# A two-layer decoder on one core: the order of TensorE, VectorE and ScalarE taken from the source instead of the scheduler

## The chip, the core and the metric

The kernel runs on one core of a Trainium2 chip. The core has several engines that run side by side, each with its own list of instructions: TensorE (PE; matmuls and transposes, with its weight loads listed apart as PEld), VectorE (DVE), ScalarE (ACT), GpSimd (POOL) and SyncE (SP, which here issues most of the transfers). Each works through its own list and waits on the others through semaphores. The metric is the time on the device in microseconds (us), and the lower it is, the better.

## The reference

The input is x, four sequences of 512 tokens with 512 features: 2048 tokens, which the kernel holds as 16 tiles of 128 tokens in 32-bit floats. There is a context of 4 × 512 × 256 and a position for each token. Two layers of three sub-layers follow one another, each with its residual and a layer normalisation after it:

```python
x = layernorm(x + L0_attn(x))         # 64 heads of 8, softmax attention
x = layernorm(x + L0_xattn(x, ctx))   # attention of the context with itself, applied to x
x = layernorm(x + L0_ffn(x))          # 8 experts, 2 a token, a shared expert and a core product
x = layernorm(x + L1_attn(x))         # 16 heads of 128, 4 key heads, rotary, causal
x = layernorm(x + L1_xattn(x, ctx))   # 32 heads of 16, rotary by position
x = layernorm(x + L1_ffn(x))          # gate, up and down with weights rounded to -1, 0, 1
```

The last sub-layer quantises activations too. Its core:

```python
def _quant_act(x):
    s = jnp.max(jnp.abs(x), axis=-1, keepdims=True) / 127.0 + EPS
    return jnp.clip(jnp.round(x / s), -128.0, 127.0), s

gate = jax.nn.silu(_qlinear(x, w_gate))      # 512 -> 2048
up = _qlinear(x, w_up)                       # 512 -> 2048
return _qlinear(gate * up, w_down)           # 2048 -> 512
```

Here `_qlinear` multiplies the rounded activations by the rounded weights and then by both scales, so the largest absolute value of a token's whole row has to be known before its row can be rounded and multiplied.

## The kernel before, in words

The whole program is one function, `decoder_kernel`, with nested functions for the stages. It opens pools of buffers and then issues the stages in turn. It is written for a tile framework: the source calls operations on tiles, and the framework finds which operation depends on which and sets the waits. It also has a scheduler, which chooses each engine's order from the operations that are ready; in the kernel before nothing limits it, so that the order in which an engine runs its instructions is the scheduler's and differs from the source's in places. The transfers of SP follow the operations that they belong to.

The stages, with the lines that matter below:

- **l0_attn** (16 pairs of a batch and two heads at a time on a strip): scores of the next pair, transposes of this one and projections of the one after are interleaved by hand in the source. At the end of a batch come `add_projection` (matmuls at L160, additions into the residual at L292) and `layernorm` (L219 and L220 statistics of four tiles, L222 the square root on ACT, L223 the reciprocal, L226 four normalisations on DVE).
- **l0_xattn**, for each batch: project the context to queries (evacuated at L431 by DVE) and keys, `softmax_scores` (L347 to L349 and the like), transpose the residual, transpose the probabilities, `add_projection`, `layernorm`.
- **l0_ffn**: routing for each batch with many small DVE operations, lists of tokens for each expert in DRAM, then the experts. After them the expert results are gathered by POOL (L817) into rows, `core(2)` and `core(3)` add the core product of two batches (L292), and `finish(b)` adds a token's two results, ACT's L827 and then DVE's L828, before the up-projection and `layernorm`. `finish(0)` runs before the next stage and the other three inside it.
- **l1_attn**: 64 heads in turn. In the source, head n issues for i = 0..3 the scores of head n+1 (matmul L900, mask L901, maxima L902, exponential L904 on ACT), one query matmul of head n+2 (L887), and one transpose group of head n (L917, copied out by DVE at L920 or ACT at L922); then `values` (four matmuls L932). The rotation of a query takes three DVE operations, L857 to L859, and one of POOL, L860, which the scores of the next head but one wait for. Every fourth head has a key matmul too, and every fourth an output projection.
- **l1_xattn**: 128 steps in the source, with two halves each. A step issues first-pass scores five steps ahead (L1116, L1132 are the two kinds of score matmul), their row maxima on DVE (L1120), exponentials on ACT (L1136) and values (L1143). A plan in the source puts all other work at a step and one of three places in it (EARLY, MIDDLE, LATE): rotations (POOL L1097, L1099), projections, the layer normalisation of a finished batch, and the quantisation of the last stage's weights: sums L998 on DVE, roundings L1016 on DVE, L1017 on POOL, L1018 on ACT, one half chunk at a time.
- **l1_ffn**: for each of 16 tiles `first(t)` and `second(t)`, issued by `pipelined` as first(0), first(1), second(0), first(2), second(1) and so on.

Of the last stage the source is, cut to what issues instructions, with the profile's line numbers:

```python
# first(t)
quantize(X[t], tmp(), xq, s)     # DVE L1305 max, L1306, L1308, L1309 round; ACT L1310 to bf16
flipped(xqt, xq, 4)              # PE L1316 four transposes; DVE L1317 copy
for n in range(4):
    mm(pg, ...); mm(pu, ...)     # PE L160, four matmuls each
    A.activation(g, pg, AF.Silu, scale=gs)                              # ACT L1334
    V.scalar_tensor_tensor(h[n], pu, us, g, ALU.mult, ALU.mult)         # DVE L1335
# second(t)
for n in range(4): V.tensor_reduce(part[:, n:n + 1], h[n], ...)         # DVE L1341
# L1342 to L1344: three small DVE operations
for n in range(4): V.tensor_scalar(h[n], ...); A.activation(hq[:, n, :], ...)   # DVE L1347, ACT L1348
flipped(hqt, hq, 16)             # PE L1316 16 transposes; DVE L1317 four copies
mm(po, chunks(hqt), wd)          # PE L160, 16 matmuls
V.scalar_tensor_tensor(X[t], po, ds, X[t], ...)                         # DVE L1355
```

After every fourth tile a `layernorm` and four stores to the output follow.

Of the kernel before, what the change touches and what calls it, by code (L numbers as in the profile page):

```python
# [85 lines left out]
@with_exitstack  # L86
def decoder_kernel(ctx: ExitStack, tc: tile.TileContext, a: dict, out: bass.AP):
    nc = tc.nc
    wp = ctx.enter_context(tc.tile_pool(name="weights", bufs=10))
    xp = ctx.enter_context(tc.tile_pool(name="resid", bufs=1))  # L90
    cp = ctx.enter_context(tc.tile_pool(name="const", bufs=1))
# [1304 lines left out]
def build(arrays):  # L1396
    import concourse.bacc as bacc

    nc = bacc.Bacc("TRN2", target_bir_lowering=False, num_devices=1)
    args = {k: nc.dram_tensor(f"in_{k}", v.shape, mybir.dt.from_np(v.dtype), kind="ExternalInput").ap()  # L1400
            for k, v in arrays.items()}
    out = nc.dram_tensor("out_0", (T, F), F32, kind="ExternalOutput").ap()
    with tile.TileContext(nc) as tc:
        decoder_kernel(tc, args, out)
    return nc
# [9 lines left out]
```

## Time and profile before

| | |
|---|---|
| time, three runs | 3037.61 us median (3037.56 to 3045.76) |
| the profiled execution: its time, its span | 3051.64 us, 3049.9 us |
| mean granted clock of TensorE | 0.967 |
| busy: PE, DVE, ACT, POOL | 2851.6, 1770.6, 1061.9, 342.5 us |
| instructions in the span | 30386 |
| HBM read, written | 82.76 MB, 46.92 MB |

The profile is of one execution; its span is the time from the first to the last recorded instruction, and its own time is 14 us above the median. Busy times count what an engine executes, without waiting. The granted clock is what the throttle gave TensorE, as a share of full speed.

In the lines quoted below, a group reads: line, engine, operation, what it writes and from what, shape, number, then busy time and mean ns of one, then the idle time of the engine just before these instructions and what ended most of it. A timeline line reads: start in us, us until the end of the last of them, engine, line, operation, shape, number, and in brackets the idle time before and what ended it. A stage's line reads: the stretch and its length, busy time and number of instructions of PE, weight loads, DVE, ACT and POOL, the clock granted, and the share and rate of the transfers.

### The profile page before, as it was taken

Reading aid. Unit: us, or ns where it says so; the run is one execution under the profiler, and the core shown is the slowest. Engines: PE = TensorE matmul, PEld = TensorE weight load, DVE = VectorE, ACT = ScalarE, POOL = GpSimd, SP = SyncE. Lnnn points to the kernel's source line nnn. Section 1 sums busy time; section 2 is a strip of 40 time slices with the busy share of each in tenths; the row PEclk is TensorE's granted clock in tenths of the full one; section 3 lists DMA queues with packets and bytes.
Section 4 is the critical chain, followed back from the end, with each engine's and each line's share of the span. In section 5 each row is a group of like instructions: output and inputs, shape, how many; then the busy total and the mean of one; then the engine's idle time right before and its main releaser. Section 6 shows DMA issues by size and latency. Waiting matters only on the chain.

```text
span 3049.9 us, 30386 instructions
## 1 busy us (share of the span) xinstructions
PE 2851.6 (93%) x11514; PEld 1370.0 (45%) x11514; DVE 1770.6 (58%) x3585; ACT 1061.9 (35%) x1945; POOL 342.5 (11%) x294
## 2 busy tenths in 40 slices
PE   7999998998798899999999999999899998998988
PEld 3444444565455345545545555533233343332444
DVE  4565455443111477757766766755655655564898
ACT  2343243233112222323322232334545444444444
POOL 3000000042002201101100100111212012110000
PEclk9999998989999899999999999999899898999999
DMA  9600001013312120000000001200201100000000
GB/s 374 266 15 1 18 11 35 11 39 115 122 38 77 55 83 1 1 1 1 1 1 1 1 28 35 90 1 15 90 1 42 63 1 28 1 15 1 1 28 28
DMA packets 56454, 131.85 MB, mean 43 GB/s; under 512 B 4810, under 2 KB 24027, under 8 KB 50147
## 3 DMA queue, kind: packets, MB, share of 16 engines
q1 hardware_dynamic: 53218, 121.31, 10.9%
q0 software_dynamic: 3072, 8.39, 0.8%
q8 instruction: 99, 1.62, 0.2%
q14 instruction: 65, 0.52, 0.1%
HBM read 82.76 MB, written 46.92 MB: 43 GB/s over the span
## 4 chain that ended last, share of the span: by engine, by line
PE 52%; DVE 10%; POOL 2%; issue 2%; DMA 1%; ACT 1%; POOLq 0%; DVEq 0%; ACTq 0%; SPq 0%
PE ps_m L160 19%; PE ps_b L1116 7%; PE ps_m L887 6%; PE ps_s L900 5%; PE ps_m L1143 4%; PE ps_b L1132 2%; PE ps_t L917 2%; PE ps_m L932 2%; POOL q L860 1%; DVE maxes L1120 1%; DVE P L1335 1%; PE ps_m L1095 1%; DMA w<-in_L_ffn_downT 1%; PE ps_s L160 1%; DVE tmp L859 1%
## 5 line engine op out<-in xcount | busy, mean ns | idle before, releaser
L160 PE MATMUL ps_m<-w,attnT 128*128 128x512 f32 (+2 forms) x1216 | 446.0, 517 | 12.3 <-issue 8.0
L1120 DVE TENSOR_REDUCE maxes<-ps_b 128x2 f32<-128x1024 f32 x256 | 311.1, 1222 | 244.5 <-PE ps_b L1132 223.6
L1136 ACT ACTIVATE PT<-ps_b 128x1024 f32<-128x1024 f32 x256 | 261.5, 1024 | 313.5 <-PE ps_b L1132 312.9
L1132 PE MATMUL ps_b<-q,k 32*128 32x512 f32 x1024 | 306.4, 678 | 33.3 <-DVE maxes L1120 33.3
L1116 PE MATMUL ps_b<-k,q 32*128 32x512 f32 x1024 | 310.3, 665 | 0.9 <-DVE maxes L1120 0.5
L160 PEld LDWEIGHTS ps_m<-w,attnT 128*128 128x128 f32 x960 | 182.9, 193 | 193.0 <-issue 177.3
L887 PE MATMUL ps_m<-xT,w 128*128 128x512 f32 x512 | 260.3, 592 | 0.0
L292 DVE TENSOR_TENSOR x<-x,ps_m 128x512 f32<-128x512 f32 x128 | 88.0, 688 | 247.5 <-PE ps_m L160 244.6
L904 ACT ACTIVATE P<-ps_s,nmax 128x512 f32<-128x512 f32 (+3 forms) x256 | 135.2, 529 | 233.5 <-DVE nmax L902 232.4
L900 PE MATMUL ps_s<-k,q 128*128 128x512 f32 (+3 forms) x512 | 183.4, 441 | 18.4 <-POOL q L860 18.1
L1116 PEld LDWEIGHTS ps_b<-k,q 32*128 32x128 f32 x1024 | 87.1, 193 | 177.4 <-issue 141.0
L860 POOL TENSOR_TENSOR q<-tmp 128x512 f32<-128x512 f32 x64 | 81.3, 1270 | 750.8 <-DVE tmp L859 714.8
L932 PE MATMUL ps_m<-PT,v 128*128 128x512 f32 (+3 forms) x512 | 162.0, 439 | 2.4 <-DVE PT L920 2.3
L349 ACT ACTIVATE P<-ps_s,nmax 128x512 f32<-128x512 f32 x128 | 88.5, 693 | 204.1 <-DVE nmax L347 204.1
L1143 PE MATMUL ps_m<-PT,vv 128*32 128x512 f32 x1024 | 148.8, 655 | 5.8 <-ACT PT L1136 5.7
L160 PE MATMUL ps_m<-w,xT 128*128 128x512 f32 (+1 forms) x384 | 144.8, 533 | 8.1 <-DVE xT L235 4.2
L911 DVE TENSOR_SCALAR P<-P,sums 128x512 f32<-128x512 f32 (+3 forms) x256 | 145.5, 571 | 4.6
L932 PEld LDWEIGHTS ps_m<-PT,v 128*128 128x128 f32 x512 | 89.0, 190 | 103.5 <-issue 49.7
L917 PEld LDWEIGHTS ps_t<-kc,P 128*128 128x128 f32 x640 | 84.0, 141 | 114.3 <-issue 84.3
L327 PE MATMUL ps_m<-xT,w 128*128 128x512 f32 x256 | 122.2, 604 | 11.1 <-DMA w<-in_L_attn_Wq 11.1
L902 DVE TENSOR_REDUCE nmax<-ps_s 128x1 f32<-128x512 f32 (+3 forms) x256 | 125.2, 490 | 5.1
L160 PE MATMUL ps_m<-xT,w 128*128 128x256 f32 (+1 forms) x384 | 124.9, 463 | 0.8 <-DVE x L292 0.8
(266 smaller groups left out, 4290.9 us busy)
## 6 DMA issues: line engine op xcount, KB each, us to landing
hidden<-w SPq DMA_DIRECT2D x16, 1024.0 KB, 18.8
result<-w SPq DMA_DIRECT2D x16, 1024.0 KB, 19.0
w<-in_L_ffn_gateT SPq DMA_DIRECT2D x8, 1024.0 KB, 4.9
w<-in_L_ffn_upT SPq DMA_DIRECT2D x8, 1024.0 KB, 4.8
w<-in_L_ffn_downT SPq DMA_DIRECT2D x8, 1024.0 KB, 5.1
w<-in_L_attn_Wqkv SPq DMA_DIRECT2D x6, 1024.0 KB, 6.0
w<-in_L_attn_Wo SPq DMA_DIRECT2D x5, 1024.0 KB, 9.2
result<-P SPq DMA_DIRECT2D x18, 256.0 KB, 2.1
```

Of the source, the lines that this page charges most:

```text
L160: PE.matmul(ps, lhsT=x, rhs=y, start=(i == 0), stop=(i == n - 1))
L887: PE.matmul(ps_q[n], lhsT=wq[h // 4][:, i, tk(h % 4)], rhs=st["xt"][:, i, :], start=(i == 0), stop=(i == 3))
L900: PE.matmul(s[:, :w], lhsT=q[:, tk(qi)], rhs=k[:, :w], start=True, stop=True)
L904: A.activation(p[:, :w], s[:, :w], AF.Exp, bias=nmax[:, qi:qi + 1], accum_out=sums[:, qi:qi + 1])
L911: V.tensor_scalar(p[:, :w], p[:, :w], sums[:, qi:qi + 1], None, ALU.mult)
L917: PE.transpose(pt[:, tk(qi)], probs[qi][:, tk(c)], ident)
L932: PE.matmul(av[:, c * P:], lhsT=st["v"][:, c, tk(g)], rhs=pts[c][:, c * P:], start=(c == 0), stop=(c == 3))
L1116: PE.matmul(s[:, j, :], lhsT=q[strip(i), tk(qi)], rhs=k[strip(i), :], start=True, stop=True)
L1120: V.tensor_reduce(at[:, 2 * half:2 * half + 2, 16 * (1 - g % 2)], s, AX.X, ALU.max, negate=True)
L1132: PE.matmul(s[:, j, :], lhsT=k[strip(i), tk(c)], rhs=q[strip(i), :], start=True, stop=True)
L1136: A.activation(p, s, AF.Exp)
L1143: PE.matmul(avs[g][strip(i), :], lhsT=vv[c][:, 4 * m + i, 16 * par:16 * par + 32], rhs=pts[g, c, i // 2][:, i % 2, :], start=(c == 0), sto ...
```

## The change

One line is added at the top of the program. It tells the framework that the instructions of three engines, TensorE, VectorE and ScalarE, are to stay in the order in which the source issues them. The scheduler still places waits and buffers, and still orders POOL and SP.

```diff
 def decoder_kernel(ctx: ExitStack, tc: tile.TileContext, a: dict, out: bass.AP):
     nc = tc.nc
+
+    ctx.enter_context(tc.manual_schedule(engines={nc.tensor.engine, nc.vector.engine, nc.scalar.engine}))
     wp = ctx.enter_context(tc.tile_pool(name="weights", bufs=10))
     xp = ctx.enter_context(tc.tile_pool(name="resid", bufs=1))
```

The set of instructions on PE, DVE, POOL and SP stays the same; ACT has six table loads fewer. In the new order 1571 of PE's 9295 instructions stand elsewhere, by 1.6 places in the mean and mostly in l1_ffn, and 2822 of DVE's 3853, by 7.9 places in the mean. On POOL 54 of 360 move, all in l1_xattn.

## The prediction

> **What bounds the kernel now.** I read the engines' shares and the slices first, then the groups with what ended their idle time, then a table by stage (the stages cut by the lines that run in them), and last the timelines of the stages in which the order changes. On the page:
>
> ```profile
> PE 2851.6 (93%) x11514; PEld 1370.0 (45%) x11514; DVE 1770.6 (58%) x3585; ACT 1061.9 (35%) x1945; POOL 342.5 (11%) x294
> PE   7999998998798899999999999999899998998988
> DVE  4565455443111477757766766755655655564898
> ...
> L1132 PE MATMUL ps_b<-q,k 32*128 32x512 f32 x1024 | 306.4, 678 | 33.3 <-DVE maxes L1120 33.3
> L900 PE MATMUL ps_s<-k,q 128*128 128x512 f32 (+3 forms) x512 | 183.4, 441 | 18.4 <-POOL q L860 18.1
> L860 POOL TENSOR_TENSOR q<-tmp 128x512 f32<-128x512 f32 x64 | 81.3, 1270 | 750.8 <-DVE tmp L859 714.8
> ```
>
> TensorE (PE) bounds: 2851.6 of 3049.9 us busy, so some 198 us idle. The largest idle sums belong to two waits, on the row maxima of l1_xattn (33.3 us) and on the rotated queries of l1_attn (18.4 us). DVE is at 8 or 9 tenths only in the last three slices. The table by stage (us; then busy us of PE, weight loads, DVE, ACT, POOL with their instructions, then PE's granted clock):
>
> ```profile
> 0.00:460.00 460.00, 437.56 (x1548) 191.60 (x1549) 244.86 (x484) 156.47 (x367) 24.54 (x24) 1.00 0.29 113
> 460.00:580.00 120.00, 109.19 (x306) 53.50 (x305) 62.68 (x120) 32.83 (x61) 0.00 (x0) 0.89 0.09 29
> 966.00:1026.00 60.00, 44.37 (x92) 18.43 (x92) 20.92 (x42) 9.61 (x18) 30.39 (x32) 0.89 0.44 147
> 1026.00:1950.00 924.00, 902.81 (x2934) 472.29 (x2935) 632.84 (x1506) 267.03 (x711) 98.99 (x78) 1.00 0.05 18
> 1950.00:2830.00 880.00, 822.60 (x4264) 320.82 (x4264) 504.37 (x647) 400.61 (x498) 136.09 (x112) 0.95 0.07 25
> 2830.00:3050.00 220.00, 191.07 (x1091) 93.27 (x1089) 196.14 (x497) 98.83 (x156) 0.00 (x0) 0.99 0.05 20
> ```
>
> The rows are l0_attn, l0_xattn, gathering with core(2) and core(3), l1_attn, l1_xattn, l1_ffn. The last row decides: PE is busy 191 and DVE 196 of 220 us. Two engines can both be that full only if their work overlaps, which is a matter of order. One tile of its loop:
>
> ```profile
> 2867.11 1.04 PE L160 MATMUL ps_s<-w,q 128*128 128x512 bf16 x4 [0.66 <-DVE q L1317]
> 2869.12 0.75 DVE L1335 SCALAR_TENSOR_TENSOR P<-ps_m,one,tmp 128x512 f32<-128x512 f32 x1 [0.40 <-PE ps_m L160]
> 2869.90 0.69 DVE L1341 TENSOR_REDUCE part<-P 128x1 f32<-128x512 f32 x1
> ...
> 2873.96 0.48 DVE L1309 TENSOR_SCALAR tmp<-x,one 128x512 f32<-128x512 f32 x1
> 2874.03 0.61 PE L1316 MATMUL ps_t<-identb,v 128*128 128x128 bf16 x8
> ...
> 2880.02 1.04 PE L160 MATMUL ps_s<-w,q 128*128 128x512 bf16 x4 [0.66 <-DVE q L1317]
> ```
>
> A tile takes 2880.02 − 2867.11 = 12.91 us. DVE puts a reduction of the tile before (L1341) between the gate multiplications (L1335), and rounds the next tile (L1309) while the present matmuls run: the scheduler's mixture.
>
> [...] half clock follows 3.4-us windows in which PE was busy for about 0.55 or less and lasts one or two windows, up to six; l0_xattn and l1_xattn show it at 0.89 and 0.95, l1_ffn hardly (0.99).
>
> **The change, part by part.** No operation is added or removed but six ACT table loads. PE, DVE and ACT keep the source's order; SP hardly moves, and POOL only in l1_xattn, where L1017 and the rotations L1097 and L1099 change places. I cost each stage against the profiled execution (3051.64 us, span 3049.9).
>
> *l1_ffn.* On DVE the source has for tile t: quantise (L1305–1309), copy (L1317), four L1335, then for tile t−1 four L1341, three small operations, four L1347, four copies and L1355; only then quantise t+1. Nothing is left to mix. From the start of the 32 gate and up matmuls, with durations of the tile above: eight groups 0.865 apart, landed at 7.1; last L1335 ends 8.0; four L1341 at 0.60, 10.4; three small ones at 0.19, 11.0; L1347 to ACT 0.58, L1348 0.62, to PE 0.06: transposes from 12.25. The four L1348 follow 0.55 apart, so the last transposes end at 14.3; 16 down matmuls (3.46) until 17.75; L1355 (0.74) 18.5. Then L1305 0.72, L1306 and L1308 0.38, L1309 to ACT 0.57, L1310 0.63, four transposes 0.46, copy and hops 0.55, in all 3.3: next matmuls at 21.8. That is +8.9 a tile. Two gaps of PE (5.15 us, and about 4.05 with 0.4 of transposes in it) come in each tile, both long enough by the clock's pattern; one and a half windows at half clock each, half of 5.1 us lost, less where PE would wait anyway: estimate +2.25 and +2.5. Period 26.6 us (21.8 if the clock stays full, 28.5 with two windows each).
> The stage: layernorm(3) in one piece (6 us) and the first quantising (3.3) put the first matmuls at 2840; tile 1 follows at 2851.6 (8.0 + 3.3, nothing to down-project yet). Tile 15: 2851.6 + 14 × 26.6 + three layernorms of 6 on the path = 3242. Then 18.5 + 2.4 for the second half of tile 14, 12 for that of tile 15, 6 for the layernorm, 2.5 for the store: 3283 against 3050, **+233** (162 at full clock, 262 at two windows).
>
> *l1_attn.* At the end of a head the scheduler put one query (L887) or key matmul ahead of the last value matmul (L932), which waits for the copy L920 behind the three rotations L857–859 (2.1 us), and ahead of the scores that wait for POOL's L860 (1.27 us). In source order that matmul is gone from the gap: 0.87 of cover in half of the 64 heads, about 0.7 in the others: **+50** (20 to 55). The three finish() and layernorm(0), (1) stand as blocks on DVE (L828, L292, L219–226, 6 us or so): **+10** (0 to 20).
>
> *l1_xattn.* PE's order is nearly the same. DVE's is not: the scheduler bunched the FFN weights' reductions (L998, 1.21 us) and roundings (L1016, 0.82 us) two to five in a row, ahead of the maxima. PE was busy 28.7 of 37 us at 2140–2177, 37.8 of 47 at 2345–2392 and 37.8 of 47 at 2550–2597, at a clock of 0.77 to 0.78. The source spreads them one in two steps. In those stretches 26.7 us are idle and at most 29 lost to the clock (a mean of 0.78 means 44% of the time at half). Against it: three layernorms in one piece, +3 each, and ACT's rounding L1018 blocked behind POOL. **−45** (−75 to 0).
>
> *l0_xattn.* Four additions and the layernorm stand in one piece ahead of the next batch's query evacuation (L431); PE now runs the next batch's projections in between. About 4.4 us a batch and 2.5 of clock: **+28** (15 to 40). *l0_attn*: layernorm delays the first copy of turned probabilities, three times 4 to 5: **+10** (0 to 20). *Routing in l0_ffn*: some 25 small DVE operations per batch (7 to 9 us) in one piece: **+15** (5 to 30). *Experts*: order practically unchanged, 0. *Gathering*: DVE's L828 waited for gathers (one in 2.5 us) ahead of core's additions (L292), PE idle 3.37, 2.19, 4.67 and 2.04; source order adds first: **−17** (−20 to −10).
>
> Sum: 233 + 50 + 10 − 45 + 28 + 10 + 15 − 17 = +284. 3051.6 + 284 = 3336 profiled; the median of the runs lies 14 below the profiled time before, so 3322.
>
> **Rivals.** (a) *Serial, but at full clock.* l1_ffn +162: 3322 − 71 = 3251. For it: before, windows as low as 0.63 there kept the clock. Against: the gaps of 4 to 5 us are longer than any there now. (b) *Half clock for two windows after each gap of l1_ffn, and the other stages near their upper ends*: 29 more there, and some 60 of the 104 that lie between the other stages' values and their upper ends, 3411. For it: runs of up to six windows occur. Against: after a gap 7 us of matmuls follow. (c) *The spreading in l1_xattn decides, not slower.* At most 57.4 us of idle time and 44 of clock (5% of 880) can come back there, 17 in the gathering: 118. It decides once l1_ffn grows by less than 118 / 16 = 7.4 us a tile and the other losses fail; at 6 a tile, 3038 − 118 + 96 = 3016. Against: 8.9 follows from measured durations and a fixed order. (d) *The order is not imposed on DVE*: 3038. Against it: in the new order DVE's instructions of l1_ffn do stand in the source's blocks.
>
> **Numbers.** Forecast 0.66, (a) 0.14, (b) 0.15, (c) 0.03, (d) 0.02. Predicted 3322 us. Leaving out one in ten at each end gives 3210 to 3415. About 0.3%, 9 us, is what can be told from no change: faster 0.03 (c), same 0.02 (d), slower 0.95.
>
> **What would show it.** l1_ffn: matmul groups of neighbouring tiles 26 to 27 us apart, L1341 four in a row, PE's clock there about 0.8 instead of 0.99, DVE's share below 6 tenths. l1_attn heads 0.7 to 0.9 longer. l1_xattn: L1132's wait on L1120 well under 33 us and a clock above 0.95. Gathering: additions before L828. The prediction is wrong if l1_ffn's period stays under 20 us, or if l1_xattn gets slower.

## The result, and the profile after

| | before | after |
|---|---|---|
| median of four runs | 3041.69 us (3037.56 to 3048.22) | 3315.10 us (3311.97 to 3318.97) |
| profiled execution, its span | 3051.64, 3049.9 us | 3318.97, 3317.2 us |
| mean granted clock | 0.967 | 0.947 |

The changed kernel is slower: its time is 1.0897 times that of the kernel before, 95% interval 1.0870 to 1.0924. Predicted were 3322 us.

The page of the changed kernel, its shares and slices and the groups that answer to those shown of before. All line numbers have moved by two: L1134 was L1132, L902 was L900, L934 was L932.

```profile
PE 2899.0 (87%) x11493; PEld 1392.7 (42%) x11514; DVE 1784.9 (54%) x3585; ACT 1045.3 (32%) x1939; POOL 335.3 (10%) x294
PE   8999987888798889999999999999999899865665
DVE  4455544441113666666666666566666655445555
...
L1134 PE MATMUL ps_b<-q,k 32*128 32x512 f32 x1024 | 296.6, 657 | 16.1 <-ACT PT L1138 8.1
L934 PE MATMUL ps_m<-PT,v 128*128 128x512 f32 (+3 forms) x512 | 166.7, 449 | 40.5 <-DVE PT L922 40.5
L902 PE MATMUL ps_s<-k,q 128*128 128x512 f32 (+3 forms) x512 | 183.5, 441 | 20.1 <-POOL q L862 18.5
```

Of the value matmuls the page of the kernel before has this line:

```profile
L932 PE MATMUL ps_m<-PT,v 128*128 128x512 f32 (+3 forms) x512 | 162.0, 439 | 2.4 <-DVE PT L920 2.3
```

Busy times hardly moved: DVE is busy 1784.9 us instead of 1770.6, PE 2899.0 instead of 2851.6. What moved is when. l1_ffn filled the last three slices before, with PE and DVE at 8 and 9 tenths. It fills the last five now, with PE at 5 and 6 and DVE at 4 and 5: both engines are nearly half idle, because they take turns. In l1_xattn the wait of L1134 on the row maxima has fallen from 33.3 us to 8.0, beside 8.1 on ACT. In l1_attn the value matmuls (L934) wait 40.5 us instead of 2.4, for the copy L922.

The table by stage, for gathering, l1_attn, l1_xattn and l1_ffn in the changed kernel (columns as before):

```profile
1006.00:1056.00 50.00, 41.05 (x95) 18.01 (x94) 15.61 (x31) 4.11 (x7) 30.59 (x32) 0.93 0.55 182
1056.00:2057.00 1001.00, 926.94 (x2939) 475.18 (x2940) 640.07 (x1509) 264.89 (x723) 98.71 (x78) 0.99 0.04 14
2057.00:2894.00 837.00, 789.91 (x4247) 311.68 (x4246) 504.36 (x639) 399.24 (x497) 131.32 (x112) 0.97 0.08 29
2894.00:3317.00 423.00, 249.41 (x1083) 113.00 (x1102) 218.74 (x516) 100.39 (x157) 0.00 (x0) 0.83 0.03 10
```

The last stage took 220 us and takes 423; l1_xattn took 880 and takes 837. One tile of l1_ffn, from the timeline of the changed kernel:

```profile
2967.30 1.89 PE L162 MATMUL ps_s<-w,q 128*128 128x512 bf16 x4 [0.52 <-DVE one L1327]
...
2976.08 0.75 DVE L1337 SCALAR_TENSOR_TENSOR P<-ps_m,one,tmp 128x512 f32<-128x512 f32 x1 [0.97 <-PE ps_m L162]
2976.74 2.46 DVE L1343 TENSOR_REDUCE part<-P 128x1 f32<-128x512 f32 x4
...
2979.81 1.67 DVE L1349 TENSOR_SCALAR P<-P,one 128x512 f32<-128x512 f32 x4
...
2981.02 2.23 PE L1318 MATMUL ps_t<-identb,v 128*128 128x128 bf16 x16 [5.04 <-ACT v L1350]
...
2987.28 0.75 DVE L1357 SCALAR_TENSOR_TENSOR x<-ps_m,one,x 128x512 f32<-128x512 f32 x1 [3.51 <-PE ps_m L162]
2987.95 0.68 DVE L1307 TENSOR_REDUCE one<-x 128x1 f32<-128x512 f32 x1
...
2990.31 0.40 PE L1318 MATMUL ps_t<-identb,tmp 128*128 128x128 bf16 x4 [3.07 <-ACT tmp L1312]
...
2991.22 1.89 PE L162 MATMUL ps_s<-w,q 128*128 128x512 bf16 x4 [0.52 <-DVE one L1327]
```

The four reductions stand in a row after the last multiplication (2976.74), the next tile's quantisation (L1307) starts only when this tile's last addition (L1357) is through, and PE is idle 5.04 and 3.07 us. The period is 2991.22 − 2967.30 = 23.92 us. After the shorter gap the first matmul group takes 1.89 us for four matmuls, where 1.03 is usual, and after the longer one the 16 transposes take 2.23 us, where 1.96 is the time of the same 16 in the run called warm below. The clock's record has a stretch of 3.41 us at half clock at both places.

**Where the 267 us of span came from.** The start of one and the same instruction in both traces, at the border of each stage, gives the shares (us, before and after):

| border (line before) | before | after | behind | in the stage | predicted |
|---|---|---|---|---|---|
| l0_attn: first L431 | 460.3 | 465.1 | +4.8 | +5 | +10 |
| l0_xattn: transposes of the first hidden() | 581.8 | 606.3 | +24.5 | +20 | +28 |
| routing: first L656 | 732.2 | 765.4 | +33.2 | +9 | +15 |
| experts: first L809 | 966.1 | 1009.4 | +43.3 | +10 | 0 |
| core(2), core(3): first L832 | 1014.9 | 1040.6 | +25.7 | −18 | −17 |
| finish(), l1_attn: last L932 | 1990.7 | 2099.2 | +108.5 | +83 | +60 |
| l1_xattn: last L1143 | 2812.7 | 2876.9 | +64.2 | −44 | −45 |
| l1_ffn: last L226 | 3045.4 | 3312.7 | +267.3 | +203 | +233 |

### The profile page after: what moved, and what is told of

Its sections match the earlier page's. It is cut to its first block, busy times and chain, and to the rows that moved or that the text cites. A ratio compares the mean times of both kernels' runs of the same rounds, so it can differ in the third digit from the quotient of the medians.

```text
span 3317.2 us, 30393 instructions
## 1 busy us (share of the span) xinstructions
PE 2899.0 (87%) x11493; PEld 1392.7 (42%) x11514; DVE 1784.9 (54%) x3585; ACT 1045.3 (32%) x1939; POOL 335.3 (10%) x294
## 5 line engine op out<-in xcount | busy, mean ns | idle before, releaser
L1134 PE MATMUL ps_b<-q,k 32*128 32x512 f32 x1024 | 296.6, 657 | 16.1 <-ACT PT L1138 8.1
L1118 PE MATMUL ps_b<-k,q 32*128 32x512 f32 x1024 | 289.2, 649 | 2.3 <-ACT PT L1138 1.8
L934 PE MATMUL ps_m<-PT,v 128*128 128x512 f32 (+3 forms) x512 | 166.7, 449 | 40.5 <-DVE PT L922 40.5
L902 PE MATMUL ps_s<-k,q 128*128 128x512 f32 (+3 forms) x512 | 183.5, 441 | 20.1 <-POOL q L862 18.5
L1118 PEld LDWEIGHTS ps_b<-k,q 32*128 32x128 f32 x1024 | 79.7, 187 | 166.0 <-issue 119.3
L1145 PE MATMUL ps_m<-PT,vv 128*32 128x512 f32 x1024 | 140.7, 622 | 4.8 <-ACT PT L1138 4.8
L934 PEld LDWEIGHTS ps_m<-PT,v 128*128 128x128 f32 x512 | 88.0, 191 | 132.2 <-DVE PT L922 65.0
L162 PE MATMUL ps_m<-PT,w 128*128 128x512 f32 (+1 forms) x248 | 118.4, 609 | 17.3 <-ACT turns L455 7.2
L903 DVE TENSOR_TENSOR ps_s<-ps_s,kc 128x128 f32<-128x128 f32 x256 | 75.2, 294 | 98.7 <-PE ps_s L902 98.6
```

Of the source, the lines that this page charges most:

```text
L162: PE.matmul(ps, lhsT=x, rhs=y, start=(i == 0), stop=(i == n - 1))
L902: PE.matmul(s[:, :w], lhsT=q[:, tk(qi)], rhs=k[:, :w], start=True, stop=True)
L934: PE.matmul(av[:, c * P:], lhsT=st["v"][:, c, tk(g)], rhs=pts[c][:, c * P:], start=(c == 0), stop=(c == 3))
L1118: PE.matmul(s[:, j, :], lhsT=q[strip(i), tk(qi)], rhs=k[strip(i), :], start=True, stop=True)
L1134: PE.matmul(s[:, j, :], lhsT=k[strip(i), tk(c)], rhs=q[strip(i), :], start=True, stop=True)
L1145: PE.matmul(avs[g][strip(i), :], lhsT=vv[c][:, 4 * m + i, 16 * par:16 * par + 32], rhs=pts[g, c, i // 2][:, i % 2, :], start=(c == 0), sto ...
```

## The experiments

All ratios are to runs of the kernel before on the same chip. The diffs are cut to the lines that matter. "In the trace" means a difference of the starts of one instruction, as in the table above.

### One stage at a time

The order of the source is imposed on a part of the program by opening and closing the same context around it: around l1_ffn's loop alone (only_ffn), on everything but that loop (all_but_ffn), around the steps of l1_xattn alone (only_xattn).

```diff
-        pipelined(range(T // P), first, second)
+        with tc.manual_schedule(engines={nc.tensor.engine, nc.vector.engine, nc.scalar.engine}):
+            pipelined(range(T // P), first, second)
```

```diff
-    run()
+    with tc.manual_schedule(engines={nc.tensor.engine, nc.vector.engine, nc.scalar.engine}):
+        run()
```

> Source order on the three engines in l1_ffn's loop alone, the scheduler's everywhere else. My theory (l1_ffn is slow because its own source order is serial, 24.0 us a tile where the scheduler had 12.9): about 200 us above the kernel before, some 3240, with 24 us a tile. Rival (the loop is slow because of what the source order does earlier, its weights or buffers coming late): within 60 us of the kernel before.

> Source order everywhere but in l1_ffn's loop. If the stages add up, as my sum assumed: the kernel before plus the 64 us that the changed kernel had lost by the end of l1_xattn, some 3105. If stages do not add up (the scheduler's l1_ffn lived on work that it pulled across the border), 3130 or more.

> Source order in the steps of l1_xattn alone. My theory (the scheduler's bunches of weight quantisation ahead of the row maxima are undone): 45 us below the kernel before, some 2995, PE's clock in the stage above 0.98 and no half-clock stretch of several windows. Rival (the 47 us that the changed kernel won back in that stage came from the different start that l1_attn gave it): less than 15 us below.

Measured: only_ffn 3238.78 us, 1.0637 times before (1.0603 to 1.0670), 24 us a tile. all_but_ffn 3140.32 us, 1.0308 (1.0276 to 1.0340). only_xattn 3005.69 us, 0.9873 (0.9843 to 0.9904): **faster than both kernels**, 1.3% faster than the one before.

The loop's loss is its own: with everything ahead of it as before, it still loses 187 us in the trace. l1_xattn's gain is its own too: 50 us in the trace, PE's clock 0.98 in the stage. One part of the expectation failed: half-clock stretches of two and three windows remain, though none of five or six as before. The same group and the stage's line, from the profile of only_xattn:

```profile
L1132 PE MATMUL ps_b<-q,k 32*128 32x512 f32 x1024 | 292.2, 649 | 16.1 <-ACT PT L1136 8.1
```

```profile
1945.00:2776.00 831.00, 787.93 (x4262) 313.82 (x4261) 509.00 (x650) 398.61 (x497) 131.22 (x112) 0.98 0.09 29
```

These two lines are also where the gain comes from. Against the kernel before, PE's idle time in the stage fell from 57.4 us (880.00 − 822.60) to 43.1 (831.00 − 787.93), by 14 us. The wait on the maxima alone fell by more, but waits on ACT took part of its place. The larger part is the clock: its record has 25 windows of 3.41 us at half clock in the stage before and 9 in only_xattn, and 16 × 3.41 / 2 = 27 us. Some 8 of the 50 us are in neither.

The expectation for all_but_ffn failed: 3140, not 3105, and so on the side of stages that do not add up. But the reason given for that side, work pulled across the border of l1_ffn, fits 7 us at most, which were lost at the start of l1_ffn. In the trace 84 us were lost by the end of l1_xattn, not 64. 19 of these 20 arose between the experts and finish(0), in an order that is the same as the changed kernel's; they are taken up below.

### Which engine's order makes the loop serial

In l1_ffn's loop alone, the source's order is kept on DVE only (ffn_vector) or on PE only (ffn_tensor).

```diff
+        with tc.manual_schedule(engines={nc.vector.engine}):      # ffn_tensor: {nc.tensor.engine}
             pipelined(range(T // P), first, second)
```

> The scheduler's order everywhere but on DVE in l1_ffn's loop, which keeps the source's. Theory (DVE's order alone makes the loop serial: the next tile's quantisation stands behind this tile's last operation): within 15 us of source order on all three engines in the loop, some 3235. Rival (PE's order is what holds the transposes and the next tile's matmuls back): below 3120.

> The scheduler's order everywhere but on PE in l1_ffn's loop, which keeps the source's. Theory (DVE's order is the cause): within 40 us of the kernel before, some 3060, a tile below 15 us. Rival (PE's order): above 3180.

Measured: ffn_vector 3239.53 us, 1.0633 (1.0596 to 1.0670), the same as all three engines (3238.78). ffn_tensor 3054.96 us, 1.0035 (1.0023 to 1.0048), with 13.7 us from tile to tile. The stage in ffn_tensor:

```profile
2826.00:3053.00 227.00, 189.25 (x1065) 93.92 (x1084) 198.53 (x497) 98.75 (x156) 0.00 (x0) 0.99 0.05 19
```

DVE's order by itself gives the whole loss. PE's source order costs some 11 us while the scheduler mixes DVE's work. ACT's order was not tried alone.

### What half clock costs in the loop

PE gets matmuls of no use in both gaps of a tile, so that it is not idle there (warm). The output does not use them.

```diff
+            keep_warm(22)
             flipped(hqt, hq.rearrange("p n c -> p (n c)"), 16)
             po = psm()
             mm(po, chunks(hqt), wd)
+            keep_warm(13)
```

```diff
+        def keep_warm(n):
+            ps = psm()
+            for _ in range(n):
+                PE.matmul(ps, lhsT=wd[0][:, :P], rhs=wg[0][:, :512], start=True, stop=True)
```

> The changed kernel with idle matmuls of no use in PE's two gaps of each tile of l1_ffn: 22 ahead of the 16 transposes and 13 after the down product, into a buffer that nobody reads (at 0.216 us each 4.75 and 2.8 us, inside gaps of 5.05 and 3.1). Theory (serial DVE work sets 21.8 us a tile, half clock the 2.2 above it): period 21.8 to 22.2, clock in the stage 0.99, in all some 30 us below the changed kernel. Rival (PE's clock costs nothing here, the chain through DVE and ACT is 24 us by itself): no gain, or a few us slower.

Measured: 3283.00 us (3274.98 to 3284.75), 32 below the changed kernel's 3315.10; the clock over the stage 0.96 instead of 0.83 (0.99 was expected). From the timeline of warm, one tile:

```profile
2960.40 1.04 PE L162 MATMUL ps_s<-w,q 128*128 128x512 bf16 x4 [0.52 <-DVE one L1332]
...
2967.31 4.91 PE L1324 MATMUL ps_m<-w 128*128 128x512 bf16 x22
2972.53 1.96 PE L1318 MATMUL ps_t<-identb,v 128*128 128x128 bf16 x16 [0.30 <-ACT v L1355]
2977.77 2.97 PE L1324 MATMUL ps_m<-w 128*128 128x512 bf16 x13
...
2981.92 1.04 PE L162 MATMUL ps_s<-w,q 128*128 128x512 bf16 x4 [0.52 <-DVE one L1332]
```

The tile takes 2981.92 − 2960.40 = 21.52 us: more work on PE, and less time. The serial chain is 21.5 us (predicted 21.8), and half clock adds 2.4 (predicted 4.75). Compared piece by piece with the changed kernel's tile, 1.6 us of it fall on the gate and up matmuls and 0.8 on the transposes and the down product.

### Is a fixed order slow in itself?

The loop's source is interleaved by hand and kept in that order: in mix_all the rest of the program is as in the changed kernel, in xattn_mix as in only_xattn. The core of both, for tile t:

```diff
-            # first(t): quantize, transposes, gate and up; second(t - 1): four maxima, rounding, 16 transposes, down
+            h, part = gate_up(xqt, gs, us, ...)      # each L1335 is followed by its L1341
+            hq, ds = round_h(h, part)                # L1342 to L1348 of the same tile
+            # mix_all: quantise t + 1 after the third group; its transposes; down(t - 1); 16 transposes of t
+            # xattn_mix: quantise t + 1 ahead of the first L1335; down(t - 1); transposes of t + 1; 16 of t; add t - 1
```

> Source order on the three engines everywhere, as in the changed kernel, but l1_ffn's source itself is interleaved by hand: each maximum follows its multiplication, the next tile is quantised after the third group of a tile, and the down product of the tile before follows the gate and up products; statistics of the layer normalisation are taken tile by tile. Theory (what costs is the order, not that it is fixed): 12.6 to 13.5 us a tile, PE's clock there 0.97 or more, in all some 3100. Rival (a fixed order is slow in itself, since an engine cannot evade a late input): above 16 us a tile, above 3150.

> Source order in the steps of l1_xattn and in l1_ffn's loop, the scheduler's elsewhere. The loop is interleaved by hand a second time: the next tile is quantised ahead of a tile's first multiplication and its transposes stand behind the down product; the addition into the residual stands last. Theory (where the first hand order lost was the transposes of the next tile, which stood on PE ahead of the down product before their input was there): 12.6 to 13.4 us a tile, in all within 12 us of only_xattn, either side. Rival (a fixed order on three engines cannot reach the scheduler's): above 14.5 us a tile, 25 us or more above only_xattn.

Measured: mix_all 3201.97 us, 1.0499 (1.0462 to 1.0536), a tile 16.5 us in the mean with the layer normalisations: the expectation failed, by 102 us. 22 of these were lost ahead of the loop, most of them where all_but_ffn lost its 19. The timeline of the loop shows what went wrong there:

```profile
3053.48 0.40 PE L1318 MATMUL ps_t<-identb,tmp 128*128 128x128 bf16 x4 [2.13 <-ACT tmp L1312]
3053.71 5.09 PE L162 MATMUL ps_m<-w,attnT 128*128 128x512 bf16 x15
```

The transposes of the next tile stood ahead of a down product that could have run, and waited for ACT: 33.0 us in 14 tiles. In nine of these tiles the clock fell for the down product behind the wait (5.09 us for 15 matmuls here, where 15 took 3.40 in warm). xattn_mix, with the transposes behind the down product, took 13.8 us a tile in the mean with the layer normalisations (the scheduler's loop in only_xattn 13.3) and 13.0 in most tiles without one. The mean is above the 12.6 to 13.4 expected. In all it took 3017.27 us, 0.9909 (0.9877 to 0.9941): 11.6 above only_xattn, within the bound but on its slower side. So a fixed order as such is not slow. That the early transposes are what made mix_all slow is read from their waits; the two hand orders also differ in where the quantisation and the last addition stand, and no run moves the transposes alone.

### l1_attn: the matmul that covered the wait

attn_query moves the first query matmul of a later head ahead of the last value matmul of this one, in the changed kernel.

```diff
             for c in range(4):
+                if c == 3 and n + 3 < len(heads) and h != 13:
+                    queries(n + 3, 0)
                 PE.matmul(av[:, c * P:], lhsT=st["v"][:, c, tk(g)], rhs=pts[c][:, c * P:],
...
-                if n + 2 < N:
+                if n + 2 < N and (i or n + 2 not in ps_q):
                     queries(n + 2, i)
```

> The changed kernel with one line of l1_attn's source moved: the first query matmul of a later head is issued ahead of the last value matmul of this head instead of after the next scores, as the scheduler had it. Theory (that matmul covered the wait of the last value matmul for its copy behind the three rotations, and the wait for POOL's sum): 0.8 us a head less in 61 heads, some 50 us below the changed kernel. Rival (the time goes to the rotations themselves, wherever the matmul stands): less than 15 us below.

Measured: 3285.87 us (3285.05 to 3286.52), 29 below the changed kernel, 32 in the trace by the end of the stage: between the 50 of the theory and the 15 of the rival. From its page:

```profile
L902 PE MATMUL ps_s<-k,q 128*128 128x512 f32 (+3 forms) x512 | 183.8, 441 | 20.1 <-POOL q L862 18.5
L936 PE MATMUL ps_m<-PT,v 128*128 128x512 f32 (+3 forms) x512 | 166.0, 448 | 4.8 <-DVE PT L922 4.7
```

The wait of the last value matmul fell from 40.5 to 4.8 us, the one on POOL's sum stayed at 20.1 (the kernel before had 18.4). Of my two waits only the first was opened by the change. Heads are still some 0.3 us longer than before; the scheduler's other moves there, key and projection matmuls in half of the heads, were not rebuilt.

### l1_xattn: is it the bunching?

In the kernel before, the scheduler had put such work in rows ahead of the row maxima, as here three sums of weights:

```profile
2152.24 3.46 DVE L998 TENSOR_REDUCE part<-w 128x1 f32<-128x1024 f32 x3
```

bunched is only_xattn with the plan of the weight quantisation altered, so that in the source's order four sums or four roundings stand in a row. The roundings of POOL and ACT that belong to them move along.

```diff
-                    plan(at + 4 * c + 2 * i, LATE, f, c, i)
+                    plan(at + 8 * (c // 2) + 6, LATE, f, c, i)
```

> Source order in the steps of l1_xattn alone, as in only_xattn, but the plan in the source puts the weights' sums and roundings of two chunks at one step, four in a row, instead of one in every second step. Theory (rows of such operations ahead of the row maxima are what the scheduler's order lost time by): 25 to 60 us slower than only_xattn, with PE idle and half clock where they stand, so about the kernel before or slower. Rival (other moves in the stage made the difference, DVE makes up for a row of four): within 10 us of only_xattn.

Measured: 3053.41 us, 1.0028 (1.0015 to 1.0041): 48 above only_xattn, and the whole gain is gone. A row of four, the group and the stage in its profile:

```profile
2175.96 4.29 DVE L1016 TENSOR_SCALAR w<-w,wi 128x1024 f32<-128x1024 f32 x4
```

```profile
L1132 PE MATMUL ps_b<-q,k 32*128 32x512 f32 x1024 | 302.3, 672 | 29.7 <-DVE maxes L1120 21.6
```

```profile
1949.00:2825.00 876.00, 810.67 (x4264) 320.15 (x4263) 518.16 (x650) 400.93 (x497) 137.64 (x112) 0.95 0.08 28
```

PE is idle 65.3 us in the stage (876.00 − 810.67) against 43.1 in only_xattn, and 24 windows of 3.41 us are at half clock in its record against 9. (65.3 − 43.1) + 15 × 3.41 / 2 = 48: idle time and clock in about equal parts. Of the 29.7 us that L1132 waits, 21.6 are waits on the maxima.

### l0_xattn, and a wait that the order does not explain

l0x_ahead is the changed kernel with the next batch's projections issued ahead of the layer normalisation; late_gathers is l0x_ahead with the gathers tied to a copy of their indices that DVE makes after core(3).

```diff
         add_projection(b, chunks(xt), pts)
+        ahead = l0_xattn_start(b + 1) if b + 1 < B else None      # projections, L431
         layernorm(b)
```

```diff
+        core(2)
+        core(3)
+        late = [cp.tile([P, T // P], I32, tag=f"late{k}", name="late") for k in range(2)]
+        for k in range(2):
+            V.tensor_copy(late[k], slots[k])
         results = {}
...
-                                             ap=slots[k][:, 4 * b + t:4 * b + t + 1], axis=0))
-        core(2)
-        core(3)
+                                             ap=late[k][:, 4 * b + t:4 * b + t + 1], axis=0))
```

> The changed kernel with the next batch's projections of l0_xattn and their evacuation issued ahead of this batch's layer normalisation. Theory (the evacuation of the queries behind the layer normalisation's block on DVE is what costs the stage 4 us a batch): a batch's period falls from 35 to 31 us, some 12 to 15 us below the changed kernel in the trace at the stage's end. Rival (the block itself delays the next batch's transposes just as much): less than 4 us.

> The kernel of l0x_ahead, which lost some 29 us between the second core product and finish(0): three of the additions of core(3) stood 5.6, 17.5 and 5.7 us idle in its trace, long after their matmuls by the profile, while POOL issued its 32 gathers. Here the gathers take their indices from copies that DVE makes behind the last addition, so that they start after it. Theory (the transfers of the gathers delay what tells DVE that PE is done): the eight additions follow 3.4 us apart, no idle time above 3 us among them; finish(0) then waits for its eight gathers instead, some 14 us behind the last addition, so that the total is 5 to 20 us below l0x_ahead. Rival (the gathers have nothing to do with it): idle times of 5 us and more among the additions again, and a total some 14 us above l0x_ahead.

Measured: l0x_ahead 3336.04 us, 1.0951 (1.0916 to 1.0986), 21 *above* the changed kernel. The fourth batch's L431 stands 6.3 us earlier, but that is the operation that was moved. At the end of the stage DVE's first copy of the transposes of hidden() starts at 605.7 us instead of 608.3: 2.6 us ahead, where 12 to 15 were expected and less than 4 by the rival. The theory failed: that the query evacuation (the copy L431, which takes the projected queries off PE's result buffer) stands behind the layer normalisation is not what costs this stage its 20 us. The rival, that the block of the layer normalisation itself delays the next batch, fits, but no run isolates it. Later the run lost 19 us where all_but_ffn had lost them. The last additions of core(3) in its timeline:

```profile
1031.00 0.69 DVE L294 TENSOR_TENSOR x<-x,ps_m 128x512 f32<-128x512 f32 x1 [5.58 <-remote]
1049.22 0.69 DVE L294 TENSOR_TENSOR x<-x,ps_m 128x512 f32<-128x512 f32 x1 [17.54 <-remote]
1055.56 0.69 DVE L294 TENSOR_TENSOR x<-x,ps_m 128x512 f32<-128x512 f32 x1 [5.65 <-remote]
```

The additions start a regular 3.43 us apart in the changed kernel, in warm and in attn_query, but not here, in all_but_ffn or in mix_all. POOL issues the 32 gathers from 1010.3 to 1050.2 meanwhile. late_gathers, whose first gather starts at 1034.44, behind the last addition:

```profile
1029.45 0.69 DVE L294 TENSOR_TENSOR x<-x,ps_m 128x512 f32<-128x512 f32 x1 [2.74 <-PE ps_m L162]
1032.88 0.69 DVE L294 TENSOR_TENSOR x<-x,ps_m 128x512 f32<-128x512 f32 x1 [2.75 <-PE ps_m L162]
...
1077.65 0.69 DVE L237 COPY xT<-ps_t 128x512 f32<-128x512 f32 x1 [12.57 <-remote]
```

The additions are regular again, as the theory had it, and the stall has moved with the gathers (1034 to 1074), to a copy of transposes at the start of l1_attn. ACT's copy of the same transposes (L239) stands idle 10.63 us there too. So nothing was gained in all: 3336.33 us, 1.0963 (1.0922 to 1.1004), where 5 to 20 less than l0x_ahead were expected. That late waits on PE come with the gathers is shown by this one move; what causes them, and why three kernels of the same order there are spared, stays open.

## Why the prediction was right, point by point

The time (3315 for 3322), the sign and the main mechanism were right. That the total came within 7 us was luck in part, as the terms below show.

- *l1_ffn serial on DVE*: right, and DVE alone (ffn_vector). The sum of durations gave 21.8 us a tile; warm, at a clock of 0.96 in the stage, measured 21.5. The sum takes each engine to keep to its list even while a later instruction could run. The changed kernel's trace shows that on DVE: it is idle 3.51 us ahead of L1357, with the next tile's L1307 behind it.
- *Half clock in both gaps*: it came in both, but its size was off: +4.75 predicted, 2.4 measured, so that matmul groups of neighbouring tiles are 24 us apart and not 26 to 27. The step that failed was one and a half windows at half clock after each gap. The record shows one, and more only at the layer normalisations (three windows) and the ends of the stage (two). After the shorter gap that window costs 1.6 us, nearly half of 3.41; after the gap ahead of the 16 transposes only 0.8, and a likely reason is that PE waits for ACT's roundings there anyway. From the first to the last tile the sum had 402 us and the trace has 367; the start and the end of the stage took 5 more than in the sum. These are the 30 us between +233 and +203. Rival (a), no clock loss, is ruled out by the 0.83 of the stage and by warm; rival (b), two windows, by the record.
- *l1_attn +50*: 48 heads from the ninth on take 0.86 us more each, 55 for 64. The wait behind the rotations was right; the wait on POOL's sum was there before as after (18.4 and 20.1).
- *finish() as blocks, +10*: too small. What is left of the +83 is 28, beyond my range of 0 to 20. The first eight heads, in which three finish() run, took 28 us longer, where 7 come from the heads.
- *l1_xattn −45*: −44, and the cause is the one named (bunched). The gain was held far below rival (c)'s 101 because idle time remains that the maxima do not cause (8.1 us on ACT for L1134 alone).
- *Gathering −17*: −18. The four waits of PE that the prediction names for it come to 12.3 us, and it does not say where the rest of the 17 comes from.
- *l0_attn, l0_xattn, routing*: 33 for 53; each was within its range. In l0_xattn the size was about right and the cause was not shown: with the query evacuation ahead of the layer normalisation (l0x_ahead) only 2.6 us came back.
- *Experts 0*: +10. The engines' order is the same, but the waits of the transposes for fetched rows rose from 20.1 to 28.2 us.

The errors (−30 in l1_ffn, −20 in the early stages, +23 in finish() and l1_attn, +10 in the experts) cancelled in part, so the total was closer than its terms. The changed kernel is also one of those that the stall of some 20 us at the gathers spared, which nothing in the prediction foresaw.

## What to carry to other kernels

Where two engines are each nearly full, as in a stage with PE busy 191 and DVE 196 of 220 us, count the period twice: once by the busiest engine and once as a chain in the written order; the difference (12.9 against 21.5) is what a scheduler's mixture is worth there. Fix the order stage by stage, not for the program: the same line gained 41 us around l1_xattn alone and lost 192 around l1_ffn alone. Where an order is written by hand, spread the work that an engine does besides its urgent operations (48 us between bunched and only_xattn), and do not put an instruction whose input is late ahead of one that can run (33.0 us of waits in mix_all).

## What the runs showed of the hardware

The clock's record comes in windows of 3.41 us. Of the windows at full clock in the traces of the two kernels, those with PE busy for less than 0.4 were followed by one at half clock in 67 of 67 cases, between 0.4 and 0.6 in 20 of 54, between 0.6 and 0.7 in 5 of 48, and above 0.7 in 9 of 1526. In all fourteen traces together I counted 455 of 455, 136 of 336, 20 of 302 and 71 of 10799. So the prediction's 0.55 lies where half clock followed in some cases and not in others. In these traces a gap did not have to fill a window: 2.1 us of idle time inside one (0.6 × 3.41) were enough every time. In mix_all half clock followed nine of 14 waits, of 2.36 us in the mean (33.0 / 14). Matmuls without use in the gaps paid for themselves in warm (32 us of 3315).

The stalls of DVE by up to 17.54 us (l0x_ahead) behind matmuls that the profile, in which their ends are modelled, has as done, while POOL issues gathers, were new to me; they cost some 20 us and came in the traces of all_but_ffn, mix_all and l0x_ahead and not in those of the changed kernel, warm and attn_query. Their cause is open.
